# A Mamba-2 block with a ternary FFN on one core: another interleaving of the last stage

## The chip, the cores and the metric

The kernel runs on one core of a Trainium2 chip. The metric is the device time of one execution in microseconds (us). Before the change three runs gave 1174.28, 1177.25 and 1177.72 us; their median, 1177.25 us, is the time to compare with.

## What is computed

The input is x, 16 sequences of 512 tokens of 256 values, all float32. Each sequence goes through two layers, one behind the other, and no sequence needs another:

```
x  = x + layernorm(attn(layernorm(x)))        # attn(u) = u + mamba2(u)
x  = x + layernorm(ffn(layernorm(x)))
mamba2(u):
  z, xBC, dt = split(u @ in_proj_w.T)          # 512, 768, 8 columns
  xBC = silu(causal depthwise conv of width 4 over tokens + bias);  xs, B, C = split(xBC)
  dt  = softplus(dt + dt_bias);  dA = exp(dt * -exp(A_log))
  S_t = dA_t * S_(t-1) + (xs_t * dt_t) B_t     # 8 heads, S is 64 x 128 per head
  y_t = S_t C_t + D * xs_t
  y   = y * silu(z);  y = y * rsqrt(mean(y*y) + 1e-5) * norm_w
  return y @ out_proj_w.T
ffn(u): gelu(u @ ternary(W1).T + b1) @ ternary(W2).T + b2      # 256 -> 1024 -> 256
```

## The kernel before

The kernel works sequence by sequence, in software-pipelined stages. Each sequence's 512 tokens are four chunks of 128. The recurrence is computed chunk by chunk with matmuls: inside a chunk as a masked product, between chunks through a state that is carried on.

The stages that matter here are Python generators. A stage issues a few instructions, then yields a number, its share of work, and so on to its end.

- **stage_b2(b)**, the scan of sequence b. `prepare(c)` (L587) readies a chunk: PE transposes into `px` (L593) and makes `pg` (L599, L600), DVE makes `xdt`, the masked `pg`, `bT` and `mt` (L595 to L611), POOL makes `xend` (L608). Then for each chunk but the last, a state step: PE `pst` (L628), for chunk 0 a copy on ACT, for the others POOL scales the old state (L633) and DVE adds (L636). Then the output: PE `py` from `mt` and `xdt` (L644) and, but for chunk 0, from `ct` and the state (L651), DVE `y` (L657), POOL `zs` = `y` times the gate (L661), and later `squares(c)`: a square on ACT (L572) and two adds on POOL (L573, L574). At its end `root` (L576) sums the squares on PE (`pss`, L580) and takes the root through DVE (L584) and POOL (L585).
- **stage_e(b)**: three multiplications on POOL, `ct` for chunks 1 to 3 (L533). `py` of chunk c needs its `ct`.
- **stage_c1(b)**, out_proj and the two norms: `squares` of the last chunk, then for each chunk `po` on PE (L710), `att` and its statistics on DVE (L716, L719), behind chunks 1 and 3 a `shift` on POOL (L268), behind chunk 3 also `second_stream` (L692, DVE and POOL). Then `norm_f.normal` on ACT makes `x3` (L282). Then PE transposes it into `pt_f` (L736), ACT rounds it to bfloat16, `x3p` part 0 (L739), DVE takes the rest (`rests`, L740). At last ACT makes part 1 (L743) and POOL part 2 (L744).
- **stage_c2(b)**, the FFN. Its first half is eight blocks `ph` of six matmuls each (L756), two for each part of `x3p`, and a Gelu on ACT into `hT` (L762); blocks 0 and 1 are split, so that their passes over part 2 come later. Its second half is `pf` for four token chunks of 16 matmul instructions each (L790), then bias, norm, residual and the output's DMA (`finish`, L780). For every sequence but the last, the `finish` of chunks 2 and 3 is put on a list, and `ending()` (L828) issues it in the next stage.

`interleave` (L815) sets the order of issue. Each stream has a generator, its work, and a place `lo` to `hi`. The stream at the smallest place takes the next step:

```
at = [lo + (hi - lo) * done / w for _, w, lo, hi, done in live]
i = at.index(min(at))
```

The places are no times. They only fix in which order instructions are put into the queue of each engine, because the schedule of PE, ACT, POOL and DVE is manual (L853). SP issues the DMAs.

Buffers that bear on the order: `ps_tr`, two PSUM banks, holds `pg`, `pt_f` and `pss` in turn; `ps_a`, four banks, holds `px`, `pst`, `py` and the last sequence's `po`; `ps_c`, two banks, holds `ph`, `pf` and the other sequences' `po`. `x3p`, `hT`, `att` and `o` exist once.

The last but one piece of the program (L910 to L918) is the stage that is changed: scan of sequence 15, out_proj and FFN of sequence 14, out_proj of sequence 15. Behind it (L919) only the FFN of sequence 15 is left.

Of the kernel before, what the change touches and what calls it, by code (L numbers as in the profile page):

```python
# [57 lines left out]
def mamba_ffn_kernel(  # L58
# [18 lines left out]
    NB = x.shape[0]  # L77
# [16 lines left out]
    def load_x(b):  # L94
        xt = io.tile([P, NC, DM], F32, tag="xin", name=f"xin_{b}")
        nc.sync.dma_start(xt, x[b].rearrange("(c p) d -> p c d", p=P))
        xin[b] = xt
# [334 lines left out]
    def stage_t0(b):  # L432
        x1 = normed[b]
        x1T = one.tile([P, 2, L], F32, tag="x1T", name=f"x1T_{b}")
        transposed(x1T, x1, f"a{b}")
        normed[b] = x1, x1T
        yield 0.9
# [90 lines left out]
    def stage_e(b):  # L528

        s = seqs[b]  # L530
        xbc, ct = s["xbc"], s["ct"]
        for c in range(1, NC):
            nc.gpsimd.tensor_tensor(  # L533
                ct[:, c - 1], ct[:, c - 1],
                xbc[:, 5, c * P : (c + 1) * P].unsqueeze(1).to_broadcast([P, NH, P]), ALU.mult,
            )
            yield 0.7 if c == 1 else 0.15
# [137 lines left out]
    def stage_c1(b):  # L675
        s = seqs[b]
        g, x1 = s["zs"], s["x1"]
        att = one.tile([P, NC, DM], F32, tag="att", name=f"att_{b}")
        s.pop("squares")()
        rms = s["rms"]  # L680

        last = b == NB - 1
        if last:
            x2 = io.tile([P, NC, DM], F32, tag="xin", name=f"x2_{b}")
            rests = io.tile([P, NC, DM], F32, tag="xin", name=f"rests_{b}")
            rests = rests.rearrange("p c d -> p (c d)").rearrange("p (k t) -> p k t", k=2)
        else:
            x2 = one.tile([P, NC, DM], F32, tag="x2", name=f"x2_{b}")
        x3 = one.tile([P, NC, DM], F32, tag="att", name=f"x3_{b}")
        norm_c, norm_f = Norm(att, f"c{b}"), Norm(x2, f"f{b}")  # L690

        def second_stream(lo, hi):  # L692


            for c in range(lo, hi):
                nc.vector.scalar_tensor_tensor(
                    x2[:, c, :], att[:, c, :], norm_c.rs[:, c : c + 1], xin[b][:, c, :],
                    ALU.mult, ALU.add,
                )
                norm_f.stats(c)  # L700
            norm_f.offset(lo, hi)

        yield 0.05
        for c in range(NC):
            if last:
                po = ps_a.tile([P, L], F32, tag="a", name=f"po_{b}_{c}")
            else:
                po = ps_c.tile([P, L], F32, tag="c", name=f"po_{b}_{c}")
            for k in range(NJ):
                nc.tensor.matmul(  # L710
                    po[:, 0:DM], g[:, k, c * P : (c + 1) * P], wo_sb[:, k, :],
                    start=(k == 0), stop=(k == NJ - 1),
                )
            if c == 2:
                s.pop("root")()
            nc.vector.scalar_tensor_tensor(  # L716
                att[:, c, :], po[:, 0:DM], rms[:, c : c + 1], x1[:, c, :], ALU.mult, ALU.add
            )
            norm_c.stats(c)  # L719
            if c % 2 == 1:  # L720
                norm_c.shift(c - 1, c + 1)
            if c == 3:
                second_stream(0, 2)
                second_stream(2, 4)
                if b + 3 < NB:
                    load_x(b + 3)
            yield (0.1, 0.07, 0.01, 0.33)[c]
        norm_f.normal(x3, 0, 1, 2, 3)
        yield 0.22
        if not last:  # L730
            rests = one.tile([P, 2, L], F32, tag="o", name=f"rests_{b}")
        x3p = one.tile([P, 3, 2, L], BF16, tag="x3p", name=f"x3p_{b}")
        for k in range(2):
            pt = ps_tr.tile([P, 512], F32, tag="tr", name=f"pt_f{b}_{k}")
            for c in range(NC):
                nc.tensor.transpose(  # L736
                    pt[:, c * P : (c + 1) * P], x3[:, c, k * P : (k + 1) * P], ident
                )
            nc.scalar.copy(x3p[:, 0, k, :], pt)  # L739
            nc.vector.tensor_sub(rests[:, k, :], pt, x3p[:, 0, k, :])  # L740
        yield 0.12
        for k in range(2):
            nc.scalar.copy(x3p[:, 1, k, :], rests[:, k, :])  # L743
            nc.gpsimd.tensor_sub(x3p[:, 2, k, :], rests[:, k, :], x3p[:, 1, k, :])  # L744
        s.update(x2=x2, x3p=x3p, shift=norm_c.off)
# [65 lines left out]
    def chain(*stages):  # L811
        for st in stages:
            yield from st
# [14 lines left out]
    def ending():  # L828
        while endings:
            endings.pop()()  # L830
        yield 0.1
# [4 lines left out]
    E_WORK = 1.0  # L836
    A0_WORK, T0_WORK, A_WORK, A2_WORK, B1_WORK, B2_WORK = 1.0, 0.9, 18.1, 1.0, 0.5, 14.9
    C1_WORK, C2_WORK = 1.0, 24.2
# [10 lines left out]
    def run(stage):  # L849
        for _ in stage:  # L850
            pass

    with tc.manual_schedule(engines=ordered):  # L853
        nc.vector.memset(rhs_e[:, 0], 0.0)
        nc.vector.memset(lhs_e, 0.0)
        interleave(
            (
                chain(stage_a0(0), stage_t0(0), stage_a(0, FIRST, 2)),
                A0_WORK + T0_WORK + A_WORK, 0.0, 1.0,
            ),  # L860
            (exponent_constants(), 9.0, 0.1, 0.5),
            (stage_a0(1), A0_WORK, 0.04, 0.28),
            (chain(stage_sil(0), stage_a2(0)), 0.1 + A2_WORK, 0.42, 0.85),
            (scales(), 6.0, 0.55, 1.0),
        )
        run(stage_t0(1))
        run(stage_a6(0))
        interleave(
            (stage_a(1, SECOND), A_WORK, 0.0, 0.8),
            (stage_b0(0), 0.1, 0.11, 0.111),  # L870
            (stage_d(0), 0.1, 0.111, 0.112),
            (stage_b1(0, 0, NC), 4 * B1_WORK, 0.112, 0.1121),
            (stage_b2(0), B2_WORK, 0.2, 0.9),
            (stage_e(0), E_WORK, 0.3, 0.65),
            (chain(stage_sil(1), stage_a2(1)), 0.1 + A2_WORK, 0.3, 0.75),
            (stage_a0(2), A0_WORK, 0.6, 0.85),
            (ternary(1), 4.0, 0.75, 0.95),
            (stage_a6(1), 0.1, 0.86, 0.861),
            (stage_b0(1), 0.1, 0.88, 0.881),
            (stage_b1(1, 0, 2), 2 * B1_WORK, 0.89, 0.9),  # L880
            (stage_b1(1, 2, 4), 2 * B1_WORK, 0.94, 0.98),
            (stage_d(1), 0.1, 0.95, 0.96),
            (stage_t0(2), T0_WORK, 0.96, 1.0),
        )
        for i in range(1, NB - 1):
            interleave(
                (ending(), 0.1, 0.0, 0.01),
                *([(ternary(2), 4.0, 0.1, 0.7)] if i == 1 else []),
                *([(stage_a6(i), 0.1, 0.02, 0.03)] if i > 1 else []),
                (stage_a(i + 1, BESIDE), A_WORK - 1.72, 0.0, 1.0),  # L890
                (stage_c1(i - 1), C1_WORK, 0.0, 1.0),
                (stage_e(i), E_WORK, 0.06, 1.0),
            )
            run(stage_a1(i + 1))
            second = [
                (stage_b0(i + 1), 0.1, 0.5, 0.51),
                (stage_b1(i + 1, 0, 2), 2 * B1_WORK, 0.68, 0.8),
                (stage_b1(i + 1, 2, 3), B1_WORK, 0.86, 0.9),
                (stage_b1(i + 1, 3, 4), B1_WORK, 0.95, 0.99),
            ]  # L900
            second.append((stage_c2(i - 1), C2_WORK, 0.02, 1.0))
            second.append((stage_b2(i), B2_WORK, 0.0, 0.98))
            second.append((stage_a2(i + 1), A2_WORK, 0.15, 0.5))
            second.append((stage_a5(i + 1), 1.7, 0.58, 0.66))
            second.append((stage_d(i + 1), 0.1, 0.92, 0.93))
            if i + 2 < NB:
                second.append((stage_a0(i + 2), A0_WORK, 0.6, 0.9))
                second.append((stage_t0(i + 2), T0_WORK, 0.94, 0.97))
            interleave(*second)
        run(stage_a6(NB - 1))  # L910
        interleave(
            (ending(), 0.1, 0.05, 0.06),
            (stage_e(NB - 1), E_WORK, 0.0, 0.25),
            (stage_c1(NB - 2), C1_WORK, 0.0, 0.4),
            (stage_b2(NB - 1), B2_WORK, 0.0, 0.53),
            (stage_c2(NB - 2), C2_WORK, 0.4, 0.98),
            (stage_c1(NB - 1), C1_WORK, 0.54, 1.0),
        )  # L918
        interleave((ending(), 0.1, 0.05, 0.06), (stage_c2(NB - 1), C2_WORK, 0.0, 1.0))  # L919

# [42 lines left out]
```

## Time and profile before

| what | us |
|---|---|
| median of three runs | 1177.25 |
| the profiled execution | 1172.91 |
| its span, first to last instruction | 1171.1 |
| last stage's first PE instruction (`pss`) | 1065.06 |
| first `pf` of sequence 14 | 1125.15 |
| first `ph` of sequence 15 | 1139.84 |
| PE busy in 1060 to 1080 | 16.30 of 20 |
| PE busy in 1080 to 1100 | 12.91 of 20 |
| PE busy in 1100 to 1110 | 8.00 of 10 |
| PE busy over the span | 1110.8 (95%) |

A profile row of the timeline gives the start, the time from the first start to the last end of the instructions merged in it, engine, line, operation, output and inputs, and in brackets how long the engine had stood idle and what ended that. In a row of the windows the columns are the stretch, its length, PE's busy time with the count of instructions, the granted share of PE's full clock, the DMA share and GB/s.

### The profile page before, as it was taken

Reading aid. Unit: us, or ns where it says so; the run is one execution under the profiler, and the core shown is the slowest. Engines: PE = TensorE matmul, PEld = TensorE weight load, DVE = VectorE, ACT = ScalarE, POOL = GpSimd, SP = SyncE. Lnnn points to the kernel's source line nnn. Section 1 sums busy time; section 2 is a strip of 40 time slices with the busy share of each in tenths; the row PEclk is TensorE's granted clock in tenths of the full one; section 3 lists DMA queues with packets and bytes.
Section 4 is the critical chain, followed back from the end, with each engine's and each line's share of the span. In section 5 each row is a group of like instructions: output and inputs, shape, how many; then the busy total and the mean of one; then the engine's idle time right before and its main releaser. Section 6 shows DMA issues by size and latency. Waiting matters only on the chain.

```text
span 1171.1 us, 16958 instructions
## 1 busy us (share of the span) xinstructions
PE 1110.8 (95%) x6164; PEld 727.9 (62%) x6164; DVE 849.0 (72%) x2211; ACT 568.0 (48%) x957; POOL 593.7 (51%) x706
## 2 busy tenths in 40 slices
PE   5778999999999999999999999999999999998697
PEld 2345475665757666575766757576675757667475
DVE  5597968768686876868687686868768686875552
ACT  5625546356454635645463564546346454532321
POOL 3453546355554635555463555546355554545742
PEclk9888999999999999999999999999999999999899
DMA  5101010020201102020110202011020101002000
GB/s 194 58 1 58 18 67 27 4 76 17 75 18 65 29 4 76 17 74 19 59 35 4 73 20 75 18 58 36 4 72 20 75 18 58 19 4 72 2 10 27
DMA packets 28627, 48.57 MB, mean 41 GB/s; under 512 B 6656, under 2 KB 25728, under 8 KB 26496
## 3 DMA queue, kind: packets, MB, share of 16 engines
q1 hardware_dynamic: 26992, 47.33, 11.8%
q8 instruction: 48, 0.79, 0.3%
q10 hardware_dynamic: 1552, 0.16, 0.1%
q14 instruction: 35, 0.29, 0.1%
HBM read 38.44 MB, written 9.04 MB: 41 GB/s over the span
## 4 chain that ended last, share of the span: by engine, by line
PE 83%; DVE 6%; POOL 6%; ACT 3%; DMA 1%; issue 1%; POOLq 0%; ACTq 0%; DVEq 0%
PE pf L790 20%; PE pm L323 12%; PE ph L756 12%; PE po L710 9%; PE pz L345 8%; PE py L644 5%; PE pst L628 4%; PE py L651 3%; POOL x3p L744 3%; PE pe L549 2%; DVE cv L330 1%; POOL xend L608 1%; PE pt_a L300 1%; PE px L593 1%; PE pt_f L736 1%
## 5 line engine op out<-in xcount | busy, mean ns | idle before, releaser
L790 PE MATMUL pf<-w_sb,hT 128*128 128x256 f32 x1024 | 248.8, 383 | 0.0
L330 DVE SCALAR_TENSOR_TENSOR cv<-pm,cw_sb,cv 128x511 f32<-128x511 f32 (+2 forms) x288 | 215.3, 747 | 44.8 <-ACT cv L328 36.9
L790 PEld LDWEIGHTS pf<-w_sb,hT 128*128 128x128 f32 x1024 | 189.8, 190 | 42.3 <-issue 14.3
L756 PE MATMUL ph<-x3p,w_bf 128*128 128x512 bf16 x768 | 189.0, 381 | 4.2 <-ACT x3p L743 1.7
L661 POOL TENSOR_TENSOR zs<-y,zs 128x512 f32<-128x512 f32 x64 | 81.7, 1276 | 206.9 <-DVE y L657 206.9
L323 PE MATMUL pm<-x1T,win_sb 128*128 128x512 f32 x384 | 184.1, 602 | 0.0
L762 ACT ACTIVATE hT<-ph,b_sb 128x512 f32<-128x512 f32 x128 | 87.8, 688 | 128.2 <-PE ph L756 128.2
L756 PEld LDWEIGHTS <-w_bf 128*128 128x128 bf16 x768 | 72.9, 98 | 93.8 <-issue 29.1
L553 ACT ACTIVATE mt<-pe 128x512 f32<-128x512 f32 x128 | 73.6, 595 | 110.3 <-PE pe L549 110.3
L710 PE MATMUL po<-wo_sb,zs 128*128 128x256 f32 x512 | 124.6, 388 | 0.3 <-DVE att L716 0.3
L345 PE MATMUL pz<-x1T,win_sb 128*128 128x512 f32 x256 | 123.8, 607 | 0.3 <-DVE dt L368 0.3
L328 ACT ACTIVATE cv<-pm,cw_sb 128x512 f32<-128x512 f32 x96 | 65.7, 684 | 118.7 <-PE pm L323 117.1
L323 PEld LDWEIGHTS pm<-x1T,win_sb 128*128 128x128 f32 x384 | 70.9, 193 | 71.8 <-issue 65.7
L710 PEld LDWEIGHTS po<-wo_sb,zs 128*128 128x128 f32 x512 | 95.8, 192 | 28.3 <-issue 16.9
L533 POOL TENSOR_TENSOR ct<-ct,xbc 128x1024 f32<-128x1024 f32 x48 | 113.3, 2374 | 0.0
L657 DVE SCALAR_TENSOR_TENSOR y<-xbc,dsk,py 128x128 f32<-128x128 f32 x256 | 71.2, 340 | 37.5 <-PE py L651 20.7
L644 PE MATMUL py<-mt,xdt 128*64 128x128 f32 x1024 | 97.0, 284 | 0.0
L796 DVE TENSOR_TENSOR o<-pf,b_sb 128x256 f32<-128x256 f32 x64 | 26.8, 419 | 88.2 <-PE pf L790 88.2
L349 ACT ACTIVATE zs<-pz 128x512 f32<-128x512 f32 x64 | 37.9, 592 | 93.3 <-PE pz L345 93.3
L345 PEld LDWEIGHTS pz<-x1T,win_sb 128*128 128x128 f32 x256 | 48.0, 194 | 55.9 <-issue 47.0
L611 DVE SCALAR_TENSOR_TENSOR mt<-mt,pg 128x1024 f32<-128x1024 f32 x64 | 77.6, 1212 | 0.5
L644 PEld LDWEIGHTS py<-mt,xdt 128*64 128x64 f32 x1024 | 61.3, 140 | 26.8 <-issue 11.8
(138 smaller groups left out, 1810.1 us busy)
## 6 DMA issues: line engine op xcount, KB each, us to landing
ct<-way SPq DMA_DIRECT2D x16, 1536.0 KB
xin<-in_x SPq DMA_DIRECT2D x16, 512.0 KB, 6.7
out<-o SPq DMA_DIRECT2D x30, 256.0 KB, 2.2
w_in<-in_w SPq DMA_DIRECT2D x1, 1024.0 KB
w_sb<-in_w SPq DMA_DIRECT2D x1, 1024.0 KB
win_sb<-in_w_in SPq DMA_DIRECT2D x1, 768.0 KB, 6.2
win_sb<-in_w_in SPq DMA_DIRECT2D x1, 512.0 KB
wo_sb<-in_w_out SPq DMA_DIRECT2D x1, 512.0 KB
```

The lines of the kernel that those rows point to most:

```text
L323: nc.tensor.matmul(pm, win_sb[:, k, DI + m * P : DI + (m + 1) * P], x1T[:, k, :], start=(k == 0), stop=(k == 1),)
L330: nc.vector.scalar_tensor_tensor(cv[:, j:], pm[:, 0 : L - j], cw_sb[:, m, 3 - j : 4 - j], cv[:, j:], ALU.mult, ALU.add,)
L345: nc.tensor.matmul(pz, win_sb[:, k, j * P : (j + 1) * P], x1T[:, k, :], start=(k == 0), stop=(k == 1),)
L533: nc.gpsimd.tensor_tensor(ct[:, c - 1], ct[:, c - 1], xbc[:, 5, c * P : (c + 1) * P].unsqueeze(1).to_broadcast([P, NH, P]), ALU.mult,)
L553: nc.scalar.activation(mt[:, hs, :].rearrange("p h t -> p (h t)"), pe, AF.Exp)
L611: nc.vector.scalar_tensor_tensor(mts[c], mts[c], 1.0, cbt.unsqueeze(1).to_broadcast([P, NH, P]), ALU.min, ALU.mult)
L644: nc.tensor.matmul(py[h % 2 * HD : (h % 2 + 1) * HD, j, :], xdt[:, h * HD : (h + 1) * HD], mts[c][:, h, :], start=True, stop=(c == 0),)
L661: nc.gpsimd.tensor_tensor(zs[:, :, tok], y, zs[:, :, tok], ALU.mult)
L710: nc.tensor.matmul(po[:, 0:DM], g[:, k, c * P : (c + 1) * P], wo_sb[:, k, :], start=(k == 0), stop=(k == NJ - 1),)
L756: nc.tensor.matmul(ph, w1_bf[:, k, f * P : (f + 1) * P], x3p[:, j, k, :], start=(j == 0 and k == 0), stop=(j == 2 and k == 1),)
L762: nc.scalar.activation(hT[:, f, :], ph, AF.Gelu, bias=b1_sb[:, f : f + 1])
L790: nc.tensor.matmul(pf[:, 0:DM], hT[:, f, c * P : (c + 1) * P], w2_sb[:, f, :], start=(f == 0), stop=(f == NF - 1),)
```

## The change

Only the numbers of the last stage's streams and their sequence in the call change:

```diff
         interleave(
-            (ending(), 0.1, 0.05, 0.06),
-            (stage_e(NB - 1), E_WORK, 0.0, 0.25),
-            (stage_c1(NB - 2), C1_WORK, 0.0, 0.4),
-            (stage_b2(NB - 1), B2_WORK, 0.0, 0.53),
-            (stage_c2(NB - 2), C2_WORK, 0.4, 0.98),
-            (stage_c1(NB - 1), C1_WORK, 0.54, 1.0),
+            (ending(), 0.1, 0.0, 0.01),
+            (stage_c1(NB - 2), C1_WORK, 0.0, 0.235),
+            (stage_e(NB - 1), E_WORK, 0.03, 0.16),
+            (stage_b2(NB - 1), B2_WORK, -0.02, 0.4),
+            (stage_c2(NB - 2), C2_WORK, 0.235, 0.98),
+            (stage_c1(NB - 1), C1_WORK, 0.42, 0.9),
         )
         interleave((ending(), 0.1, 0.05, 0.06), (stage_c2(NB - 1), C2_WORK, 0.0, 1.0))
```

No instruction is added or left out. `stage_c1` of sequence 14, the scan of sequence 15, the FFN of sequence 14 and `stage_c1` of sequence 15 are each issued in their own order as before, but mixed differently.

## The prediction

> **What bounds the kernel now.** TensorE (PE) is busy 95% of the span, but not in the stage that is changed. I read first PE's timeline from 1065 us on, for the waits between its instructions:
>
> ```profile
> 1073.08 1.52 PE L628 MATMUL pst<-xend,bT 128*128 128x512 f32 x2 [2.04 <-POOL xend L608]
> ...
> 1090.75 2.08 PE L628 MATMUL pst<-xend,bT 128*128 128x512 f32 x2 [3.89 <-POOL xend L608]
> ...
> 1096.87 0.63 PE L736 MATMUL pt_f<-ident,x 128*128 128x128 f32 x4 [3.19 <-DVE mt L611]
> ...
> 1103.00 0.38 PE L756 MATMUL ph<-x3p,w_bf 128*128 128x512 bf16 x1 [1.43 <-ACT x3p L743]
> ```
>
> The four brackets make 10.6 us of waiting; with smaller ones (1.67 at 1067.95, 0.34 at 1109.67, 0.22) it is 12.8 us, all for POOL, DVE and ACT. Then PE's windows of 3.4 us, the last column but two being the granted clock:
>
> ```profile
> 1066.90:1070.30 3.40, 2.35 (x13) 1.00 0.00 0
> 1070.30:1073.70 3.40, 1.36 (x9) 1.00 0.00 0
> 1073.70:1077.10 3.40, 3.40 (x9) 0.50 0.09 32
> ...
> 1101.00:1104.50 3.50, 1.84 (x16) 0.98 0.00 0
> 1104.50:1107.80 3.30, 3.30 (x28) 0.50 0.00 0
> ```
>
> Behind a window with PE busy for 1.36 or 1.84 us the next runs at half clock; behind 2.35 us it doesn't. Windows from 1090.8 and 1097.6 are at 0.51 and 0.50 too. So a wait is paid twice. Behind the stall zone:
>
> ```profile
> 1114.10:1139.80 25.70, 25.70 (x126) 1.00 0.00 1
> ```
>
> From the sixth FFN block of sequence 14 (`ph` 5, at 1114.28 in the chain of waits) PE is full at full clock. What counts is when PE reaches `ph` 5; the rest follows at a fixed distance.
>
> What holds PE before that are POOL and DVE. Each takes its instructions in the order of issue:
>
> ```profile
> 1089.65 1.04 POOL L608 TENSOR_TENSOR xend<-xdt,dec 128x512 f32<-128x512 f32 x1
> ...
> 1096.41 2.35 POOL L533 TENSOR_TENSOR ct<-ct,xbc 128x1024 f32<-128x1024 f32 x1
> ...
> 1099.93 1.04 POOL L633 TENSOR_TENSOR state<-state,dec 128x512 f32<-128x512 f32 x1
> ...
> 1105.23 2.27 POOL L744 TENSOR_TENSOR x3p<-rests,x3p 128x512 bf16<-128x512 f32 x2
> ```
>
> ```profile
> 1101.01 0.69 DVE L636 TENSOR_TENSOR state<-pst,state 128x512 f32<-128x512 f32 x1 [4.28 <-POOL state L633]
> 1101.61 1.28 DVE L740 TENSOR_TENSOR rests<-pt_f,x3p 128x512 f32<-128x512 f32 x2
> ```
>
> `rests` had its inputs at 1098.1 and stood behind `state`, which waited for POOL. POOL ran from 1088.73 to 1100.97 without a hole.
>
> **The change part by part.** Nothing is added or removed, only orders change. I worked the interleaver's places through by hand. The new order differs in these points: (a) `xend` 0 goes ahead of `ct` 1 on POOL, and the `finish` of sequence 13 (DVE, POOL, one SP DMA) stands behind `prepare(0)`; (b) `pst` 0 and `py` 0 are mixed with the four `po`; (c) `pt_f` and `rests` stand ahead of `prepare(3)`, and `x3p` part 2 on POOL ahead of `squares` 1 and `state` 2; (d) `ph` 0, `ph` 1's first passes and `ph` 0's last pass stand ahead of `py` 3; (e) from `ph` 5 on PE's order is the old one, except that sequence 15's `pt_f` comes 12 `pf` instructions earlier. I walk the queues with the durations above; the gap between two dependent instructions is in them.
>
> *Front, (a) and (b).* POOL is free at 1068.48 in both. New: `xend` 0 to 1069.45; it waits for the two `finish` steps on DVE, which follow `mt` 0 (ends 1070.33) and take 0.81: 1071.15. Then `finish` 1.26, `squares` of sequence 14 1.21, `xend` 1 1.0, `ct` 1 2.35: 1077.0. Then `shift` 0.93, `zs` 0 1.26, the power for `rms` of chunk 3 0.56: 1079.7. PE in the meantime: `pg` 0 at 1067.95 as before, `po` 0 to 1071.0, `pst` 0 to 1071.9 (no 2.04 wait, so also no half clock at 1073.7), `po` 1 1073.6, `py` 0 1074.5, `po` 2 and `po` 3 1078.1, each `po` 1.73 (its eight instructions at full clock). `att` 3 waits for `rms` and starts at 1079.75, where the trace has 1082.52: 2.8 us earlier. DVE and POOL then have the old order to `xend` 2: `second_stream` ends at 1085.8 (was 1088.56), POOL's last norm step starts at 1085.95 (was 1088.73).
>
> *POOL chain, (c).* From there POOL has no hole again: norm step 0.9, `xend` 2 1.0, `squares` 0 1.2, `state` 1 1.0, `ct` 2 2.35, `zs` 1 1.25, `ct` 3 2.35, now `x3p` part 2 2.27 (to 1098.2), then `squares` 1 1.2 and `state` 2 1.0: 1100.4, was 1100.97. So the inserted 2.27 eats nearly all of the front's 2.8.
>
> *PE beside it.* `px`, `pg`, `pst`, `py` of chunks 2, 2, 1, 1 end at 1081.5. Then PE waits for `x3`: off_f at 1086.87, ACT's last two norms 1.09: 1088.0. This is a new wait of 6.5 us, and behind it are queued all of `pt_f`, `px` 3, `pst` 2, `py` 2. At half clock `pt_f` and `px` 3 last to 1090.7. `pg` 3 needs the bank that `rests` reads; `rests` stands on DVE behind `state` 1 (1090.75) and `y` 1 (1091.85) and ends half at 1092.5, whole at 1093.1. So a second wait, to 1092.5. Then `pg` 3 0.35, `pst` 2 0.86, `ph` 0 0.86, `py` 2 1.74, `ph` 1 0.86, `ph` 0's last pass 0.43, partly at half clock: about 1099.3. `py` 3 needs `state` 2, on DVE at 1100.45 to 1101.05. PE waits again, and all that came before is hidden: slack 1.7 us. `py` 3 starts at 1101.1, was 1103.97, because `x3p` part 1 (ACT, 1093.75) no longer stands in between.
>
> *The rest.* `py` 3 takes 1.74 at full clock, 3.4 at half (old: 3.2). Then `ph` 1's last pass 0.43, three blocks of 1.3, `pss` 0.56. Here the price of the clock is open. The Trainium skill (TensorE: Matmul & The Clock Gate, "Why this matters for your kernels") warns of PE-idle gaps over about 3 us between bursts. It speaks against this change for the 6.5 us gap, which is hidden; but by it the gap before `py` 3, 1.8 us, costs nothing: `py` 3 ends at 1102.85, `ph` 3 waits for a Gelu until 1104.8 (`zs` 2 1103.4, its square 0.63, Gelu 0.69), `ph` 5 is reached at 1107.95, gain 6.3. By the row 1101.0, gaps that leave 1.84 us busy in a window halve the next; here some 1.7 to 1.9 would be busy. Then `py` 3 ends at 1104.5, `ph` 5 starts at 1109.4, gain 4.9. I take the row, which is nearer than the rule. The bounds of the unknown are one such half-clock window, 1.7 us, either way.
>
> *Tail, (e).* Sequence 15's `pt_f` moves up to 8.63 us behind the first `pf` (40 instructions of 0.2157): 1133.94 on the old times. ACT finished `x3` at 1133.73. So it fits with 0.2 us to spare; each us that DVE is later costs one. `x3p` part 2 comes about 1 us earlier than its 1141.32, but nobody waited for it. The wait of 0.40 for the first Gelu at 1143.0 stays. The `finish` DMA of sequence 13 goes out some 3 us earlier than at 1075.8, with SP's queue empty. Gain here 0, with -0.5 as the lower bound.
>
> *Sum.* Profiled execution 1172.91 (span 1171.1 and 1.8 around it) minus 4.9 is 1168.0. The median of the runs is 4.3 above that execution; I carry the saving over: 1177.25 - 4.9 = 1172.35.
>
> **Rivals.**
> 1. *Walk right, clock full at `py` 3*: gain 6.3, 1170.95. For it: where PE's free windows fall against the gap is chance.
> 2. *The front moves nothing.* POOL already waits 1.7 us for `finish` in the walk; if `state` 2 is 2.8 later than walked (DVE done 1103.85), `py` 3 ends near 1106.8 and `ph` 5 comes at 1111.7: gain 2.6, 1174.65, within 0.3%, which is what a measurement can tell from no change. Against it: `ct` 1 had blocked `xend` 0 for 2.4 us.
> 3. *Slower: the FFN stands in the scan's way.* `ph` 0's last pass is now ahead of `py` 3 on PE and needs `x3p` part 2, behind `ct` 3 on POOL. If that comes at T, `ph` 5 comes at T + 7.1 (0.43 + 1.74 + 0.43 + 3.9 + 0.56). Walked T is 1098.2; it delays from 1100.7 and makes the kernel slower from 1107.2. T near 1112, through `rests` kept back by a buffer (the output of sequence 13 is read from it), would give 1182. Against it: that DMA lands some 2 us from issue, 15 us before `rests`.
>
> **How the numbers follow.** Walk with half clock 0.45 (1172.35), rival 1 0.25 (1170.95), rival 2 0.22 (1174.65), rival 3 0.08 (1182). The runs before spread from 3.0 below to 0.5 above their median. The range goes from rival 1 less that spread, 1168, to rival 2 plus about 1.9, 1176.5; it leaves out rival 3 and the edges. Faster by over 0.3% (3.5 us): 0.36 + 0.24 + 0.05 = 0.65; slower: 0.07; same: 0.28.
>
> **What would show it.** `pst` 0 without its wait; `att` 3 near 1079.8; a new PE wait of about 6.5 us ahead of `pt_f`, released by ACT; POOL's `x3p` part 2 straight behind `ct` 3; `state` 2 on DVE within 1 us of the old time; `py` 3 near 1101, with its clock; `ph` 5 at 1109.4; from there to the end 57 us as before. It is wrong if PE waits for `x3p` part 2 past 1101, if sequence 15's `pt_f` waits for ACT, or if `state` 2 comes after 1103.

## The result, and the profile after

The changed kernel takes 1170.53 us (median of six runs, 1169.83 to 1173.17), the kernel before 1176.82 in the runs beside it. The ratio is 0.9953, its 95% interval 0.9940 to 0.9967: a gain of 5.5 us, with 3.9 to 7.1 as the bounds (the two medians alone differ by 6.3). The forecast was a gain of 4.9 us and a time of 1172.35.

The two profiled executions differ by less: their spans are 1171.1 and 1168.9. The difference lies ahead of the changed stage, in code that didn't change. PE's `pz` matmuls begin at 20.57 us before and at 24.02 after, and the last stage's first `pss` comes at 1065.06 and 1068.68. The profile of before is the odd one: in the nine experiments below that `pss` comes at 1067.88 to 1070.22. Its `xin` loads also landed sooner, in 6.7 us at the median, against 8.6 after and 8.2 to 8.7 in the experiments; that this is the cause is not shown. The lead is probably also most of the 4.3 us by which this execution lay below its median. From here on I count the **stage**: from that first `pss` to the end of the span. It was 106.04 us and is 100.22, a gain of 5.82 us. (The span is given to a tenth, so a stage time is good to about 0.05 us.)

PE's timeline after, the rows with waits from `pt_f` to `py` 3 and the rows at which `py` 3 begins:

```profile
1089.37 0.33 PE L736 MATMUL pt_f<-ident,x 128*128 128x128 f32 x1 [3.70 <-ACT x L282]
...
1091.32 1.82 PE L736 MATMUL pt_f<-ident,x 128*128 128x128 f32 x6 [1.12 <-ACT x L282]
...
1096.26 0.80 PE L599 MATMUL pg<-xbc 128*128 128x128 f32 x2 [2.27 <-DVE rests L740]
...
1104.20 0.44 PE L644 MATMUL py<-mt,xdt 128*64 128x128 f32 x4
1104.93 0.44 PE L651 MATMUL py<-ct,state 128*64 128x128 f32 x4 [0.29 <-DVE state L636]
1105.20 0.39 PE L644 MATMUL py<-mt,xdt 128*64 128x128 f32 x4
```

The waits for `xend` are gone, and new ones for `x3` (ACT) and `rests` (DVE) stand in their place. PE waits for `state` 2 only 0.29 us, and the rows of `py` 3 follow each other every 0.22 us. That is full clock; at half clock, before the change, they came every 0.43 us. On POOL the chain is the same as before, with `x3p` now inside it:

```profile
1090.58 1.04 POOL L608 TENSOR_TENSOR xend<-xdt,dec 128x512 f32<-128x512 f32 x1
...
1097.34 2.37 POOL L533 TENSOR_TENSOR ct<-ct,xbc 128x1024 f32<-128x1024 f32 x1
1099.66 2.27 POOL L744 TENSOR_TENSOR x3p<-rests,x3p 128x512 bf16<-128x512 f32 x2
...
1103.11 1.04 POOL L633 TENSOR_TENSOR state<-state,dec 128x512 f32<-128x512 f32 x1
```

On DVE `rests` now goes ahead of `state` 2, which waits for POOL:

```profile
1095.52 1.28 DVE L740 TENSOR_TENSOR rests<-pt_f,x3p 128x512 f32<-128x512 f32 x2
...
1104.18 0.69 DVE L636 TENSOR_TENSOR state<-pst,state 128x512 f32<-128x512 f32 x1 [5.32 <-POOL state L633]
```

Counted from the first `pss`, `xend` 2 begins at 21.90 (it was 24.59), but `state` 2 on DVE at 35.50 (it was 35.95). The front's lead is eaten by `x3p`, as the walk said. These are PE's windows after the change, with the granted clock in the last column but two:

```profile
1084.20:1087.60 3.40, 1.47 (x28) 1.00 0.00 0
1087.60:1091.00 3.40, 0.66 (x2) 1.00 0.00 0
1091.00:1094.40 3.40, 2.65 (x10) 0.50 0.01 2
1094.40:1097.80 3.40, 1.54 (x4) 0.50 0.01 2
1097.80:1101.20 3.40, 3.40 (x12) 0.50 0.00 0
1101.20:1104.60 3.40, 3.40 (x40) 0.99 0.00 0
```

Half clock lasts from 1091.0 to 1101.2 without a break, all of it ahead of `py` 3. The chain of waits reaches `ph` 5 at 1111.86, 43.18 us into the stage (it was 49.22), and from there the end is 57.04 away (it was 56.82).

### The profile page after: what moved, and what is told of

Read it like the earlier page. It is cut to its first block, busy times and chain, and to the rows that moved or that the text cites. A ratio compares the mean times of both kernels' runs of the same rounds, so it can differ in the third digit from the quotient of the medians.

```text
span 1168.9 us, 16958 instructions
## 1 busy us (share of the span) xinstructions
PE 1110.5 (95%) x6164; PEld 726.3 (62%) x6164; DVE 850.3 (73%) x2211; ACT 568.5 (49%) x957; POOL 594.6 (51%) x706
## 4 chain that ended last, share of the span: by engine, by line
PE 82%; DVE 7%; POOL 6%; ACT 3%; DMA 1%; issue 1%; POOLq 0%; ACTq 0%
PE pf L790 20%; PE pm L323 13%; PE ph L756 12%; PE po L710 9%; PE pz L345 8%; PE py L644 5%; PE pst L628 3%; PE py L651 3%; POOL x3p L744 3%; PE pe L549 2%; DVE cv L330 1%; POOL xend L608 1%; PE pt_a L300 1%; PE px L593 1%; PE pt_f L736 1%
## 5 line engine op out<-in xcount | busy, mean ns | idle before, releaser
L644 PE MATMUL py<-mt,xdt 128*64 128x128 f32 x1024 | 95.7, 282 | 0.0
L611 DVE SCALAR_TENSOR_TENSOR mt<-mt,pg 128x1024 f32<-128x1024 f32 x64 | 77.6, 1212 | 0.5
L644 PEld LDWEIGHTS py<-mt,xdt 128*64 128x64 f32 x1024 | 60.3, 138 | 27.5 <-issue 12.9
```

Source lines behind the costliest of these rows:

```text
L611: nc.vector.scalar_tensor_tensor(mts[c], mts[c], 1.0, cbt.unsqueeze(1).to_broadcast([P, NH, P]), ALU.min, ALU.mult)
L644: nc.tensor.matmul(py[h % 2 * HD : (h % 2 + 1) * HD, j, :], xdt[:, h * HD : (h + 1) * HD], mts[c][:, h, :], start=True, stop=(c == 0),)
```

## The experiments

All kernels ran in five rounds beside the kernel before. Stage times are from one profile each. How well they repeat can be read from parts that kernels share: with the changed front `att` 3 begins 14.75 to 14.77 us into the stage in seven profiles, and from `ph` 5 to the end the nine profiles with the changed order behind it agree within 0.1 us. So a difference of 0.4 us between two stage times is more than what repeats, but it rests on one profile each. The ratios can't show it: their intervals reach 1.1 to 1.6 us to either side, and those of most experiments overlap. The experiments step the six streams in a written-out order instead of by places: b is the scan of sequence 15, c `stage_c1` of 14, E the `ct` multiplications, f the FFN of 14, d `stage_c1` of 15, n the `ending`. The changed kernel's first 36 steps are `bncbncbEcbccb` (the front, to `prepare(2)`) and `bEbcEEcbcbfbffbfffbfbdf`.

**front_only** and **back_only** each take one half of the change.

```diff
-"bncbncbEcbccb" + "bEbcEEcbcbfbffbfffbfbdf" ...      # the change
+"bncbncbEcbccb" + "bEbEcEbbcbcfbffffbffbdf" ...      # front_only
+"Ecbcbnbnccbcb" + "bEbcEEcbcbfbffbfffbfbdf" ...      # back_only
```

> The last stage is counted from its first pss on PE to the end of the span: 106.0 us before, 100.2 after. This kernel has the new order up to prepare(2) and the old order from there. Theory (the walk: two parts, each worth about half, POOL's chain carries both): the chain to state 2 comes 2.8 us earlier than before, rests still stands behind state 2, so the stage gives 103.2 us (102 to 104.5, a half-clock window being 1.7), the ratio to before about 0.9976. Rival A (only the order of rests, x3p and pt_f behind prepare(2) matters): 106.0, ratio 1.000. Rival B (all of the gain is the front): 100.2, ratio 0.995.

Measured: stage 102.42, ratio 0.9978 (0.9968 to 0.9988).

> Old order up to prepare(2), new order from there. Theory: POOL's x3p steps (2.27 us) now come ahead of state 2, which so comes 2.3 us later than before, near 38.7 us behind the stage's first pss (before 36.4 with DVE), but py 3 no longer waits for rests and x3p part 1, so py 3 begins as before and its remainder is shorter: stage 103 us (102 to 104), ratio about 0.997. Rival A (only the back matters): 100.2, ratio 0.995. Rival B (all of it is the front): 106 or more, ratio 1.000 or above.

Measured: stage 102.85, ratio 0.9981 (0.9971 to 0.9990). Both halves gain, 3.6 and 3.2 us in the stage, where both rivals asked for all or nothing. In front_only PE still waits for the things that the back moves:

```profile
1090.86 2.07 PE L628 MATMUL pst<-xend,bT 128*128 128x512 f32 x2 [5.06 <-POOL xend L608]
...
1096.98 0.94 PE L736 MATMUL pt_f<-ident,x 128*128 128x128 f32 x4 [3.20 <-DVE mt L611]
...
1103.11 0.38 PE L756 MATMUL ph<-x3p,w_bf 128*128 128x512 bf16 x1 [1.44 <-ACT x3p L743]
```

The three brackets are those of before (3.89, 3.19, 1.43), the first one longer, for PE is there sooner. `state` 2 and `py` 3 come 2.7 us earlier than before, which is the front's lead. The rest of the 3.6 comes from the clock: `py` 3 takes 1.9 us here (1104.01 to 1105.91) where before it took 3.2, and part of that is lost again in a wait of 0.51 us for `x3p` behind it. In back_only `py` 3 is at full clock as well (1108.60 to 1110.57). So each half alone wins some 1.2 us there, and the whole change can win them only once. That is about the size of the 1.0 us by which the sum of the halves, 6.8, exceeds the whole.

**ct1_first** asks which step of the front matters.

```diff
-"bncbncbEcbccb" + ...
+"Ebncbncbcbccb" + ...
```

> The changed kernel, but ct 1 goes first on POOL, as it did before the change. Theory (POOL's sum decides, not which step is first; POOL idles 1.6 us for finish in the changed kernel, and ct 1 fills that hole): pst 0 comes 1 us later, but att 3 0.8 us earlier, and the stage is 0.8 us shorter, 99.4. Rival (the front's gain is that xend 0 no longer stands behind ct 1): the front's 2.8 us go, stage 102.5 to 103.

Measured: stage 100.21, ratio 0.9951 (0.9938 to 0.9963). There is no gain and no loss. The rival is out (that `xend` 0 stands ahead of `ct` 1 isn't the source), but the 0.8 us of my theory are missing too. DVE's timeline shows a row I had not counted on, `finish`'s two steps; the second row is what POOL runs beside them:

```profile
1074.18 1.76 DVE L290 TENSOR_SCALAR o<-o,rs_o,off_o 128x256 f32<-128x256 f32 x2
...
1074.70 1.09 POOL L608 TENSOR_TENSOR xend<-xdt,dec 128x512 f32<-128x512 f32 x1
```

The two take 0.81 us before the change and 0.73 after it. So DVE is late by 1.0 us. What was expected of the next experiment puts this down to `ct` 1. The trace doesn't bear that out: `ct` 1 ended at 1074.74, the first step took 0.71 beside its end, and the second took 1.13 beside `xend`. **ct1_first_act** takes these steps off DVE.

```diff
-            norm_o.apply(o, *range(lo, hi))
+            if b == NB - 3 and lo == 2:
+                neg = small.tile([P, NC], F32, tag="neg", name="neg", bufs=1)
+                nc.scalar.mul(neg[:, lo:hi], norm_o.off[:, lo:hi], -1.0)
+                for c in range(lo, hi):
+                    nc.scalar.activation(
+                        o[:, c, :], o[:, c, :], AF.Identity,
+                        bias=neg[:, c : c + 1], scale=norm_o.rs[:, c : c + 1],
+                    )
+            else:
+                norm_o.apply(o, *range(lo, hi))
```

> ct1_first with finish's two normalizing steps of sequence 13 on ACT (and a small negation there) instead of DVE. In ct1_first these two took 1.76 us on DVE in place of 0.73 while POOL ran ct 1. Theory (DVE's steps were held by POOL's long multiplication, and that ate the 0.8 us that ct1_first was to give): att 3 comes 0.7 us earlier, stage 99.5. Rival (something else holds the front): 100.2 as ct1_first.

Measured: stage 100.09, ratio 0.9957 (0.9944 to 0.9969). The theory fell. DVE's hold is gone (`xdt` 1 begins at 1074.30, straight behind `mt` 0), yet `att` 3 isn't earlier. This is `att` 3 after the change and then in ct1_first_act:

```profile
1083.44 0.48 DVE L716 SCALAR_TENSOR_TENSOR att<-po,rms,x 128x256 f32<-128x256 f32 x1 [0.76 <-POOL rms L585]
...
1083.78 0.48 DVE L716 SCALAR_TENSOR_TENSOR att<-po,rms,x 128x256 f32<-128x256 f32 x1 [0.68 <-PE po L710]
```

It comes 14.67 us into the stage (14.76 after the change) and waits for PE's `po` 3, no longer for POOL. In ct1_first, too, it waited 0.68 us for `po` 3. PE is late because `pst` 0 waited 0.83 us for `xend` 0. So POOL's and PE's chains to `att` 3 are nearly equal, and shortening one alone gives nothing.

**x3p_behind_state** undoes the insertion in POOL's chain.

```diff
-... "cbcbfbffbfff" ...      # rests and pt_f, prepare(3), x3p, state 2
+... "cbbcfbffbfff" ...      # x3p behind state 2
```

> The changed kernel, but x3p parts 1 and 2 of sequence 14 are issued behind squares 1, pst 2 and state 2 instead of ahead. Theory: state 2 comes 2.3 us earlier on DVE, but ph 0's last pass stands ahead of py 3 on PE and needs x3p part 2, which now ends where state 2 ended; so PE waits there, and the stage is 100.2 less 0 to 0.5 us. Rival (state 2 on POOL is the bound by itself): 97.9.

Measured: stage 99.78, ratio 0.9943 (0.9930 to 0.9957): 0.44 us less, in the bounds of the theory. DVE's `state` 2 came 2.2 us earlier, at 33.26, but `py` 3 begins at 35.81, near the old place (35.52). PE's timeline shows no bracket there, since the wait is short, but the chain of waits shows it:

```profile
1102.75 2.24 POOL x3p L744 x2
1104.98 0.04 issue
1105.03 0.38 PE ph L756
```

`ph` 0's last pass starts 0.28 us later than behind an unbroken row of `ph`, when POOL's `x3p` part 2 is done. So the theory's wait is there, but it is small, because PE itself, late from its half clock, gets to that pass only at 35.2.

**pe_kept_busy** asks what the half clock costs.

```diff
-            for m in range(4):
+            for m in 6 * [0, 1, 2, 3] if b == NB - 1 and c == NC - 1 else [0, 1, 2, 3]:
                 nc.tensor.transpose(px[:, m * P : (m + 1) * P], xbc[:, m, tok], ident)
...
+            if b == NB - 2 and k == 0:
+                for _ in range(16):
+                    nc.tensor.matmul(pt, w1_bf[:, 0, 0:P], w1_bf[:, 0, 0:512], start=True, stop=True)
```

> The changed kernel with idle PE time filled: 16 extra matmuls ahead of pt_f of sequence 14 (3.45 us at full clock, overwritten by the transposes), and the four transposes of px 3 issued six times (2.2 us more). Nothing else changes; the results are the same. It asks whether the half clock from 22.3 to 32.6 us behind the stage's first pss costs anything. Theory (it is hidden: py 3 waits for state 2 at 36.2 us in any case): PE gets there 2 us sooner, waits longer, and the stage stays at 100.2, or gets up to 1.7 us longer if the longer wait now halves the clock behind it. Rival (the half clock is paid in full): 98 or less.

Measured: stage 101.57, ratio 0.9968 (0.9957 to 0.9979): slower than the change by 1.35 us.

```profile
1102.26 0.44 PE L644 MATMUL py<-mt,xdt 128*64 128x128 f32 x4
1104.90 0.70 PE L651 MATMUL py<-ct,state 128*64 128x128 f32 x4 [2.20 <-DVE state L636]
1105.38 0.64 PE L644 MATMUL py<-mt,xdt 128*64 128x128 f32 x4
1105.80 0.64 PE L651 MATMUL py<-ct,state 128*64 128x128 f32 x4
```

PE was at full clock from `pt_f` on, reached `py` 3 1.9 us sooner, waited 2.20 us instead of 0.29, and ran `py` 3 in steps of 0.43: half clock. The first row of `py` 3 that needs `state` 2 came at the old time (36.27 against 36.25). So with POOL's chain as it is, the 10 us of half clock in the changed kernel are hidden, and being late there is even worth 1.35 us, as it keeps the wait ahead of `py` 3 short.

**x3p_on_dve** and **both**: the first makes POOL's chain shorter without any change of order, the second adds the filling of pe_kept_busy.

```diff
-            nc.gpsimd.tensor_sub(x3p[:, 2, k, :], rests[:, k, :], x3p[:, 1, k, :])
+            low = nc.vector if b == NB - 2 else nc.gpsimd
+            low.tensor_sub(x3p[:, 2, k, :], rests[:, k, :], x3p[:, 1, k, :])
```

> The changed kernel with the two subtractions that make x3p part 2 of sequence 14 on DVE, so that POOL's chain to state 2 is 2.3 us shorter. Theory (POOL's chain leads PE by only 0.3 us at py 3): py 3's wait of 0.3 goes, and PE, which is late from its half clock, becomes the bound at once: stage 99.8 (99.5 to 100.0). Rival (POOL alone is the bound): 98.0.

Measured: stage 99.68, ratio 0.9954 (0.9942 to 0.9967). The stage is 0.5 us shorter, as the theory has it, and PE's wait for `state` 2 is gone; the ratio shows no difference from the change.

> The two edits of the two kernels before together. Theory (two chains of nearly the same length end at py 3, so only both together give): py 3 starts near 33.9 us in place of 36.0, a Gelu wait takes some of it, stage 98.0 (97.6 to 98.8), ratio to before about 0.993. Rival (the clock costs nothing anywhere): as x3p_on_dve.

Measured: stage 98.79, ratio 0.9939 (0.9927 to 0.9952). Alone, the shorter chain gives 0.5 us and the filling costs 1.35; together they give 1.4, and PE is at full clock from the first `pss` to the end of `py` 3. So two chains of nearly one length end at `py` 3. The stage lies at the upper edge of the theory's range. PE now waits 1.25 us for `state` 2, since POOL gained less than the 2.3 us: its adds beside DVE's subtractions got longer. These rows are from both:

```profile
1098.92 1.17 POOL L573 TENSOR_TENSOR y<-y 128x256 f32<-128x256 f32 x1
1100.17 0.78 POOL L574 TENSOR_TENSOR sq<-y 128x128 f32<-128x128 f32 x1
...
1102.73 0.44 PE L651 MATMUL py<-ct,state 128*64 128x128 f32 x4 [1.25 <-DVE state L636]
```

After the change the two adds take 0.74 and 0.45.

**both_squares_late** takes more out of POOL's chain: the squares of a chunk are owed until the next state step has been issued.

```diff
...
+                while owed:
+                    squares(*owed.pop())
...
-                squares(c, y)
+                if b == NB - 1:
+                    owed.append((c, y))
+                else:
+                    squares(c, y)
```

> The kernel 'both' (x3p part 2 of sequence 14 on DVE, PE's idle time filled), and in the scan of sequence 15 the squares of chunks 0 and 1 issued behind the next state step instead of ahead of it. Theory (POOL's chain to state 2 is the bound again once PE is kept at full clock: py 3 waited 1.25 us for it in 'both'): the two adds of chunk 1 (1.2 to 1.9 us) leave the chain ahead of state 2, the stage goes from 98.8 to 97.5 (97.0 to 98.0), ratio to before about 0.992. Rival (PE or a Gelu is next at once): 98.3 to 98.8.

Measured: stage 97.62, ratio 0.9924 (0.9910 to 0.9937), 1167.92 us: the best version here, 8.4 us in the stage better than before. The size is in the theory's range, but POOL is not what bounds it any more. DVE's two subtractions became the long step, and PE waits for them (the line numbers are those of this kernel):

```profile
1096.96 4.17 DVE L756 TENSOR_TENSOR x3p<-rests,x3p 128x512 bf16<-128x512 f32 x2
...
1101.18 0.38 PE L768 MATMUL ph<-x3p,w_bf 128*128 128x512 bf16 x1 [1.07 <-DVE x3p L756]
```

In both they took 2.63 us. Here the first stands beside POOL's `ct` 3 and the second beside its scaling of the state, which itself took 1.49 us instead of 1.04. DVE's `state` 2 follows them without a wait for POOL.

## Why the prediction was right, and where it was not

The order of the chains was right: the front gains, `x3p` spends most of that gain on POOL, and the new PE waits are hidden behind POOL's chain. The term for the clock was wrong, and that the time still came out near the forecast is partly luck. The measured 1170.53 us lies nearer to rival 1 (1170.95) than to the walk (1172.35). The interval of the runs, 3.9 to 7.1 us, holds the gains of both, so only the trace decides between them.

*The front.* The walk put `att` 3 at 14.69 us into the stage, with no wait at `pst` 0. Measured are 14.76 and no wait. One duration was wrong almost without effect: the small `rs_c` step (L257) took 1.51 us instead of 0.17, all but its end beside POOL's `ct` 1. POOL came to its next step only 0.03 us before that step ended.

*POOL's chain.* The walk put `state` 2 on DVE at 35.39, with the inserted `x3p` eating the lead. Measured is 35.50, and front_only, whose `x3p` stands behind `state` 2, has it at 33.24.

*The new waits.* The forecast was one wait of 6.5 us ahead of `pt_f`. It is split, into 3.70, 0.16 and 1.12, as the transposes of a chunk begin once that chunk of `x3` is there. The end of `px` 3 was walked at 25.6 and came at 25.30, and `pg` 3 was walked at 27.44 and came at 27.58.

*The clock, the step that failed.* The walk took half clock in `py` 3, from the row of one window with 1.84 us busy, and so a gain of 4.9 us; with full clock it had 6.3. Measured is full clock, and `ph` 5 comes 6.0 us earlier: that is rival 1's case. Two things failed. PE's half clock ahead of `py` 3 didn't end at once but lasted over three windows, to 32.5 us into the stage, so PE came to `py` 3 at 35.5 instead of 34.2. And the first matmuls of `py` 3 (L644) don't need the state at all, so they filled part of the wait. Of the 1.8 us gap 0.29 was left.

That row was no rule either. The same place in front_only, with almost the same work and busy time, has the other outcome. The first two rows are before, the last two front_only:

```profile
1101.00:1104.40 3.40, 1.74 (x16) 1.00 0.00 0
1104.40:1107.80 3.40, 3.40 (x30) 0.50 0.00 0
...
1100.60:1104.00 3.40, 1.73 (x14) 1.00 0.00 0
1104.00:1107.40 3.40, 3.16 (x38) 1.00 0.00 0
```

(On a window of 3.40 us the prediction's 1.84 is 1.74.) After the change, too, the window behind 1.47 us busy at 1084.2 stayed at 1.00, and the one behind 2.65 us, all transposes, at 1091.0 stayed at 0.50. What is counted stays open, and so does what the walked gap of 1.8 us would have done. A gap of 2.20 us there, with 1.26 us busy in its window, does halve the clock, as pe_kept_busy shows. The Trainium skill warns of PE-idle gaps over about 3 us (TensorE: Matmul & The Clock Gate, "Why this matters for your kernels"); by this gap, and by the one of 2.04 us before the change, that figure is too generous here. One more thing is untested. The half-clock stretches of nine profiles begin 22.3 to 22.7 us into the stage or a multiple of 3.41 us from there, so no run shows the price when they fall elsewhere.

*The tail.* The forecast was 0, with -0.5 as the bound; the tail is about 0.2 us longer. Sequence 15's `pt_f` had no wait, but the margin was thinner than the prediction says: 1125.15 and 8.63 make 1133.78 and not 1133.94, so 0.05 us were left, not 0.2. Measured are just 0.05 us (`x3` ends at 1131.31, `pt_f` begins at 1131.36). What the tail lost lies at a place where the prediction saw no wait: POOL's `x3p` part 2 of sequence 15 ends at 1139.47, and the tenth `ph`, which needs it, starts at 1139.52, 0.16 us late.

*Rivals.* Rival 2 (the front moves nothing) is out by front_only. In rival 3 the new place of `ph` 0's last pass would hold `py` 3. After the change `x3p` part 2 was done at 1101.93, and that pass ran without a wait. The mechanism exists: the pass waited 0.28 us in x3p_behind_state, 0.34 in pe_kept_busy and 1.07 in both_squares_late. Its price in the changed kernel is nothing.

## What to carry to other kernels

When a stage with several engines is reordered, walk each queue by itself and ask which chain comes second: here POOL's and PE's chains met within 0.3 us at one matmul, so a shorter POOL chain alone gave 0.5 us, a faster PE alone lost 1.35, and both gave 1.4. When the second chain is shortened, a third one can take over, as DVE's did in both_squares_late. An instruction moved ahead of another on a busy in-order queue takes its full length from what stands behind it, so most of a gain at the front can be spent before the end. Count profiles that differ in their start-up from a mark inside the program, not from zero.

## What the runs showed of the hardware

Some steps of DVE took longer beside a step of POOL, and the other way round. A DVE step of 128x2 (L257) took 1.51 us in place of 0.17 beside POOL's multiplication of 2.35 us:

```profile
1079.01 1.51 DVE L257 TENSOR_SCALAR rs_c<-mv_c 128x2 f32<-128x2 f32 x1
```

Two scale-and-shift steps took 1.76 in place of 0.73, most of it beside `xend`. Not every step is touched: in ct1_first `mt` (L611) kept its 1.21 us beside the same multiplication. In the other direction, POOL's adds went from 0.74 to 1.17 and from 0.45 to 0.78 beside DVE's subtraction of two SBUF inputs, and that subtraction went from 2.63 to 4.17 for two beside POOL's `ct` 3 and its scaling of the state.

Busy time in a window did not decide PE's clock by itself: behind 1.74 us busy it was halved, and behind 1.73 us of almost the same work in another kernel it was not. And filling PE's idle time to keep its clock up made the kernel slower, as it turned hidden lateness into a wait at a worse place.
